# The first norm of five batches from an input with channels on partitions

## The chip, the cores and the metric

The kernel runs on one core of a Trainium2 chip. Time is the device time of one launch in microseconds (us). The core's engines are PE (TensorE, matmuls and transposes), DVE (VectorE), ACT (ScalarE), POOL (GpSimd) and SP (SyncE, which here only issues DMAs). "PEld" is the loading of weights into PE, which overlaps PE's matmuls.

## The reference

Eight batches of 256 tokens with 256 channels go through four layers in float32, each with a residual (`x = x + layer(x)`).

```
L0:  x = x + attention(norm1(x));  return x + swiglu(norm2(x))      16 heads of 16 channels, hidden 1024
     norm(x) = g * x * rsqrt(mean(x*x, channels) + 1e-6) + b,   g, b = linear maps of the batch's condition
L1:  attention with masked keys, then an RMS norm scaled and shifted by the condition
L2:  quaternion rotation; with the transform and its inverse it is one fixed 256 x 256 linear map
L3:  router over 8 experts, the best two; each expert is a network 256 -> 512 -> 512 -> 256
```

The change concerns `norm1` alone: the first norm of L0, for batches 3 to 7. Its mean runs over the channels of a token, so the divisor belongs to a token, while `g` and `b` belong to a channel of a batch.

## The kernel before, in words

**Layouts.** A batch `x` lies in SBUF with 128 tokens on the partitions and two token groups beside each other (128 x 2 x 256, `NQ` = 2). A matmul contracts over partitions, so the projections to queries, keys and values need the channels on partitions (`xT`, 128 x 2 x 256, `KC` = 2).

**The first norm** (`first_norm`, 1045, and `normed`, 891) works in the first layout: two Square activations on ACT with a running sum (`junk_n`, line 878), 11 small DVE instructions for the reciprocal root (`rq_..._n`, 611 to 622, no table), and two multiplications on POOL (`xs_n`, 902), one for each token group. It is a generator in three parts, which the caller starts one at a time. `first` (1053) then calls `conditioned` (908): four 128 x 128 transposes on PE (`flipped`, 884, `pt_n`) into one PSUM bank, and two DVE instructions (924) that read the bank and apply `g` and `b`, which in this layout are one number for each partition. Then come the projections (`qkv`, 937): `pk`, `pq`, `pv`, of 8 matmuls together 1.8 us each.

**Attention** has four score blocks for each batch and layer. A block (983 to 991) is four matmuls into one tile of four PSUM banks, `s_a`, and one exp on ACT over 128 x 2048 (`pe_a`, line 990). The pool of that tile has one buffer (531), so the next block's matmuls need the exp of the one before to be done. `values` (993) follows after every second block (`o_a`), with a transpose on DVE (`tu_a`). In this text `s_a_3_1_1` is the last of the four blocks of batch 3's first attention. All other results of PE go through three one-bank buffers (529).

**Order.** Batches 0 to 2 are set up first (to line 1824), with batch 3's first norm in `second_step` (1817). Then a loop for i from 2 to 6 (1829 to 1849) weaves, in each pass, eight score blocks: four of the second attention (L1) of batch i−2, then four of the first attention of batch i+1. Between the blocks `run` (1669) takes pieces from `others(i-1)` (1725): the SwiGLU of batch i−1 (`pg`, `ph`, then `pd`), with the pieces of `first(i+2)` inside, and the projections of the second attention of batch i−1 (`pk_a`, `pq_a`, `pv_a`, lines 932 and 962, from `x2T`, after another norm `n2` and its flips). A piece has a planned cost, 1.9 us unless it yields another number, and pieces are taken until their sum reaches the planned time between blocks (`gaps`). PE's order is that of this text, and so are DVE's and ACT's in the loop, all three engines' and POOL's before it. `starts` and `beside` list which parts of norms (`n1` is batch i+2's first norm), rotations and the router go to DVE, ACT and POOL at which block.

**Transfers.** SP loads `x` of batch b+3 in `after_first` (1071) and a row `mod` broadcast over the partitions in `swiglu` (1086, a ring of two buffers). The last third of the time belongs to the experts, with their weights streamed in; the change does not touch it.

## Time and profile before

| what | value |
|---|---|
| median of 3 runs | 714.43 us (713.82 to 716.17) |
| the profiled execution | 713.96 us |
| its span, first to last instruction | 712.2 us |
| PE busy | 698.3 us |
| DVE busy | 367.3 us |
| ACT busy | 256.7 us |
| POOL busy | 182.5 us |
| exp of one score block | 1877 ns, 64 of them |
| mean granted clock of PE | 0.995 |

A row of the timeline gives the start, the duration, the engine and line, the operation with output and input, the number of instructions, and in brackets how long the engine had been idle and who released it. Matmuls overlap at their ends, so the time of one piece of work is read from its start to the start of the next. A line of the waits names an engine's line, the instruction that it waited for, then the sum in us, the number of waits and the longest. In a DMA row stand the number of transfers, the size of one and the time from issue to landing.

### The profile page before, as it was taken

What the parts mean: (1) busy time and instruction counts of PE and PEld (TensorE: products, weight loads), DVE (VectorE), ACT (ScalarE), POOL (GpSimd) and SP (SyncE); (2) the same over time, 40 slices, a digit from 0 to 9 for tenths busy, and PEclk for the clock granted to TensorE, in tenths of its full rate; (3) what the DMA queues carried; (4) which work ended last, traced back from release to release, by engine and by line L of the source; (5) the groups of instructions that cost most, each with busy time, mean ns of one, the idle gap of its engine ahead of it and who ended that gap; (6) DMA issues with size and microseconds to landing.
All of it is one profiled execution on the core that took longest, in us unless ns stands there. A gap on an engine that the chain in (4) does not pass through costs nothing.

```text
span 712.2 us, 11237 instructions
## 1 busy us (share of the span) xinstructions
PE 698.3 (98%) x4300; PEld 536.7 (75%) x4300; DVE 367.3 (52%) x1165; ACT 256.7 (36%) x412; POOL 182.5 (26%) x219
## 2 busy tenths in 40 slices
PE   9999999999999999999999999999999999999994
PEld 7567776766766766766666786688888998989884
DVE  5447435575468585477584776688222222222221
ACT  4553345345355345355434235322211222221220
POOL 5302601101100140100220116224463333433113
PEclk9999999999999999999999999999999999999998
DMA  8500000000020000020000421736595765956512
GB/s 292 168 17 15 1 1 16 1 16 16 1 75 17 1 17 1 1 75 1 2 15 1 142 75 25 289 131 210 151 307 164 228 228 167 300 170 237 179 16 34
DMA packets 26624, 67.66 MB, mean 95 GB/s; under 512 B 8121, under 2 KB 20737, under 8 KB 24129
## 3 DMA queue, kind: packets, MB, share of 16 engines
q1 hardware_dynamic: 17712, 55.20, 22.3%
q0 software_dynamic: 8560, 11.46, 7.4%
q8 instruction: 36, 0.59, 0.3%
q14 instruction: 28, 0.22, 0.1%
q10 hardware_dynamic: 288, 0.18, 0.1%
HBM read 57.24 MB, written 9.59 MB: 94 GB/s over the span
## 4 chain that ended last, share of the span: by engine, by line
PE 91%; DVE 5%; ACT 1%; issue 1%; POOL 1%; DMA 0%; POOLq 0%; DVEq 0%; ACTq 0%
PE ph_a_rest L1492 13%; PE s_a L988 9%; PE pg L1096 8%; PE o_a L1001 8%; PE ph L1096 7%; PE pd L1109 7%; PE ph_s_sure L1492 6%; PE ph_a_p L1492 5%; PE pe_a_rest L1522 4%; PE pq_a L932 4%; PE pk_a L932 4%; PE py L1024 2%; PE pe_s_sure L1522 2%; PE pe_a_p L1522 2%; PE pv_a L962 2%; PE py L1142 2%
## 5 line engine op out<-in xcount | busy, mean ns | idle before, releaser
L990 ACT ACTIVATE pe_a<-s_a 128x2048 f32<-128x2048 f32 x64 | 120.1, 1877 | 107.9 <-PE s_a L988 107.7
L988 PE MATMUL s_a<-qz_a,kT_a 32*128 32x512 f32 x512 | 73.2, 639 | 1.6 <-DVE qz_a L946 1.0
L1492 PE MATMUL ph_a_rest<-h_a_rest,w_a_rest 128*128 128x256 f32 x288 | 63.7, 379 | 0.0
L1096 PE MATMUL pg<-xT_n,gate_wT 128*128 128x256 f32 x256 | 61.9, 385 | 0.0
L1001 PE MATMUL o_a<-pe_a,va 128*32 128x256 f32 x1024 | 61.9, 382 | 0.0
L1096 PE MATMUL ph<-xT_n,hid_wT 128*128 128x256 f32 x256 | 61.6, 383 | 0.0
L1001 PEld LDWEIGHTS o_a<-pe_a,va 128*32 128x32 f32 x1024 | 30.0, 109 | 39.9 <-issue 23.4
L1492 PEld LDWEIGHTS ph_a_rest<-h_a_rest,w_a_rest 128*128 128x128 f32 x288 | 54.1, 190 | 7.0
L1109 PE MATMUL pd<-out_wT,hT 128*128 128x256 f32 x256 | 59.2, 383 | 0.0
L1096 PEld LDWEIGHTS ph<-xT_n,hid_wT 128*128 128x128 f32 x256 | 47.7, 190 | 13.7 <-DVE y L1068 3.0
L1109 PEld LDWEIGHTS pd<-out_wT,hT 128*128 128x128 f32 x256 | 47.7, 190 | 12.3 <-issue 3.2
L1096 PEld LDWEIGHTS pg<-xT_n,gate_wT 128*128 128x128 f32 x256 | 47.4, 190 | 12.1 <-issue 2.5
L1503 DVE TENSOR_SCALAR h_a_rest<-ph_a_rest,w_a_rest 128x256 f32<-128x256 f32 x36 | 17.4, 484 | 73.5 <-PE ph_a_rest L1492 72.4
L1069 POOL TENSOR_TENSOR xy<-y,x 128x512 f32<-128x512 f32 x8 | 10.1, 1268 | 143.1 <-DVE y L1068 88.1
L1501 ACT ACTIVATE h_a_rest<-ph_a_rest,w_a_rest 128x256 f32<-128x256 f32 x36 | 17.1, 475 | 77.3 <-DVE h_a_rest L1503 77.3
L1010 DVE STREAM_TRANSPOSE tu_a<-o_a 128x512 f32<-128x512 f32 x32 | 22.8, 712 | 40.6 <-PE o_a L1001 40.5
L1282 POOL DMA_INDIRECT slots<-rec,posi x32 | 31.8, 995 | 31.8 <-DVE rec L1280 16.5
L1536 POOL DMA_INDIRECT out<-ye_a_rest,trec_a_rest x18 | 28.5, 1581 | 39.1 <-ACT ye_a_rest L1534 30.0
L1100 ACT ACTIVATE th<-pg 128x512 f32<-128x512 f32 x32 | 19.0, 595 | 45.8 <-PE pg L1096 45.4
L988 PEld LDWEIGHTS s_a<-qz_a,kT_a 32*128 32x128 f32 x512 | 20.2, 183 | 19.5 <-issue 12.8
L1102 DVE SCALAR_TENSOR_TENSOR sg<-th,pg 128x512 f32<-128x512 f32 x32 | 21.9, 684 | 24.0 <-ACT th L1100 24.0
L1492 PE MATMUL ph_a_rest<-xt_a_rest,w_a_rest 128*128 128x256 f32 x144 | 32.6, 379 | 0.0
(354 smaller groups left out, 1176.1 us busy)
## 6 DMA issues: line engine op xcount, KB each, us to landing
w_a_rest<-in_experts SPq DMA_DIRECT2D x9, 2180.0 KB, 9.2
w_a_p<-in_experts SPq DMA_DIRECT2D x5, 2180.0 KB, 8.7
w_s_sure<-in_experts SPq DMA_DIRECT2D x4, 2180.0 KB, 9.3
w_s_early<-in_experts SPq DMA_DIRECT2D x1, 2180.0 KB, 8.4
mod<-mod_rows SPq DMA_DIRECT2D x8, 256.0 KB, 3.3
tokens<-x SPq DMA_DIRECT2D x4, 512.0 KB, 3.2
out<-x SPq DMA_DIRECT2D x4, 512.0 KB, 4.4
x<-in_x SPq DMA_DIRECT2D x7, 256.0 KB, 2.7
```

The costliest lines, as they stand in the source:

```text
L932: nc.tensor.matmul(pp[:, c, :], w[:, k, c * P : (c + 1) * P], xT[:, k, :], start=k == 0, stop=k == KC - 1)
L988: nc.tensor.matmul(sc[:, j], kT[r, c, kc * P : (kc + 1) * P], qz[r, c], start=True, stop=True)
L990: nc.scalar.activation(pe, sc, AF.Exp)
L1001: nc.tensor.matmul(o[32 * i : 32 * i + 32, qd, :], va[:, kc, 8 * c + 4 * qd + i].rearrange("p a d -> p (a d)"), pe[:, 2 * qd + i // 2, i % ...
L1010: nc.vector.transpose(turned.rearrange("p q j a d -> p (q j a d)"), o.rearrange("p q s -> p (q s)"))
L1096: nc.tensor.matmul(ps[:, j, :], w[:, k, o : o + P], yT[:, k, :], start=k == 0, stop=k == KC - 1)
L1102: nc.vector.scalar_tensor_tensor(sg, th, 1.0, pg, ALU.add, ALU.mult)
L1109: nc.tensor.matmul(pd[:, t, :], hT[:, c, t * P : (t + 1) * P], out_w[:, c, :], start=c == 0, stop=c == HID // P - 1)
L1282: sc = nc.gpsimd.indirect_dma_start(out=slots, out_offset=bass.IndirectOffsetOnAxis(ap=posi[:, t : t + 1], axis=0), in_=rec[:, t, :], in_o ...
L1492: nc.tensor.matmul(ph[:, c - c0, 0:many], w[:, o : o + P], src[:, k, 0:many], start=k == 0, stop=k == n_in - 1,)
L1522: nc.tensor.matmul(pos[q][0:p, q, :], h2[:, k, q * p : (q + 1) * p], w[:, o : o + D], start=k == 0, stop=k == MC - 1,)
L1536: ad = nc.gpsimd.indirect_dma_start(out=out[0 : reach(n), :], out_offset=bass.IndirectOffsetOnAxis(ap=rec[0:p, q, 0:1], axis=0), in_=y[0:p ...
```

## The change

The host adds a second copy of `x` with channels on partitions. For batches 3 to 7 `first_turned` takes the place of `first_norm`: the squares and the reciprocal root are as before, but the scaling by the root works on the turned copy. There the divisor runs along a row, the same for all partitions, so the 256 roots are written to DRAM and read back as one row broadcast to 128 partitions. DVE multiplies the turned copy by it, POOL applies `g` and `b`, and `first` goes to the projections without transposes. The piece that held the flips stays in the plan with a cost of 0.0 instead of 0.6. In the loop the parts of `n1` start two blocks earlier, and in `second_step` the first two parts of batch 3's norm come one step earlier. The tile `scaled` moves to the ring of `mod`. The planned `gaps` stay as they are.

```diff
+    rstd_rows = dram.tile([B, P, NQ], F32, tag="rstd_rows", name="rstd_rows")
...
-        scaled = work.tile([P, KC, B, E], F32, tag="r_msg", bufs=1, name="scaled")
+        scaled = wt("mod", [P, KC, B, E], "scaled")
...
+    def first_turned(b):
+        s = state[b]
+        s["x"] = xs_in.pop(b)
+        ss = squares(s["x"], f"n1_{b}")
+        xT = wt("xs", [P, KC, S], f"xr_{b}", 3)
+        nc.sync.dma_start(out=xT, in_=a["xT"][b])
+        yield
+        rstd = rsqrt(work, ss, NQ, 1.0 / D, 1e-6, f"n1_{b}")
+        nc.sync.dma_start(out=rstd_rows[b], in_=rstd)
+        rows_ = wt("rb", [P, P, NQ], f"rb_{b}", 1)
+        nc.sync.dma_start(
+            out=rows_.rearrange("p t q -> p (t q)"),
+            in_=rstd_rows[b].rearrange("t q -> (t q)").partition_broadcast(P),
+        )
+        yield
+        parts = xT.rearrange("p k (q t) -> p k q t", q=NQ)
+        nc.vector.tensor_tensor(
+            parts, parts, rows_.rearrange("p t q -> p q t").unsqueeze(1).to_broadcast([P, KC, NQ, P]), ALU.mult
+        )
+        dst = s["xT1"] = wt("xT", [P, KC, S], f"xT_n1_{b}", 3)
+        for k in range(KC):
+            nc.gpsimd.tensor_scalar(
+                dst[:, k, :], xT[:, k, :], aff[:, 0, k, b : b + 1], aff[:, 1, k, b : b + 1], ALU.mult, ALU.add
+            )
+        yield
+
     def first(b):
         s = state[b]
+        if "xT1" in s:
+            yield 0.0
+            s["qkv0"] = yield from qkv(s.pop("xT1"), wq0, wk0, wv0, f"a0_{b}")
+            return
...
+            n1 = first_turned(3)
+            next(n1)
+            next(n1)
             next(rotation)
             yield
-            do(first_norm(3))
+            do(n1)
...
-        n1 = first_norm(i + 2) if i + 2 < B else iter(())
+        n1 = first_turned(i + 2) if i + 2 < B else iter(())
...
-        starts = {0: [last], 1: [last, n2], 2: [n2, n1]}
+        starts = {0: [last, n1], 1: [last, n2], 2: [n2]}
         beside = {
-            0: [last], 1: [last, n2], 2: [n1, n1], 3: [last], 4: [placed], 5: [r1], 6: [rotated],
+            0: [last, n1], 1: [last, n2], 2: [n1], 3: [last], 4: [placed], 5: [r1], 6: [rotated],
...
+        "xT": v["x"].transpose(0, 2, 1).reshape(B, KC, P, S).transpose(0, 2, 1, 3),
```

## The prediction

> **What bounds the kernel now.** I read the page's first part, the slices and the chain, then the waits of TensorE (PE), then its timeline around each place that the change touches.

> ```profile
> PE 698.3 (98%) x4300; PEld 536.7 (75%) x4300; DVE 367.3 (52%) x1165; ACT 256.7 (36%) x412; POOL 182.5 (26%) x219
> ...
> PEclk9999999999999999999999999999999999999998
> ...
> PE 91%; DVE 5%; ACT 1%; issue 1%; POOL 1%; DMA 0%; POOLq 0%; DVEq 0%; ACTq 0%
> ```

> PE is busy for 698.3 of 712.2 us at an undiminished clock, and 91% of the chain is its own work. So a change pays what it takes off PE's text order, and costs what it makes PE wait. PE has few waits (columns: us in all, times, longest):

> ```profile
> PE pt_n L888 <- POOL xs_n L902: 0.6, 1, 0.6
> ...
> PE s_a L988 <- ACT pe_a L990: 0.2, 1, 0.2
> ```

> The second line is the rule that decides this case. All score blocks share one PSUM tile, and the next block's first matmul needs the last exp (`pe_a`) to have emptied it. PE's timeline (start, duration, count) in one pass of the steady loop, and ScalarE's (ACT) exp in it:

> ```profile
> 147.87 1.14 PE L988 MATMUL s_a<-qz_a,kT_a 32*128 32x512 f32 x8
> 148.94 2.05 PE L962 MATMUL pv_a<-wv,x2T 128*128 128x264 f32 x8
> 151.01 1.14 PE L988 MATMUL s_a<-qz_a,kT_a 32*128 32x512 f32 x8
> 152.08 1.93 PE L1001 MATMUL o_a<-pe_a,va 128*32 128x256 f32 x32
> ```

> ```profile
> 149.08 1.88 ACT L990 ACTIVATE pe_a<-s_a 128x2048 f32<-128x2048 f32 x1 [3.37 <-PE s_a L988]
> ```

> From 147.87 to 151.01 are 3.14 us: 1.07 of scores (start to next start), 0.14 until the exp begins, 1.88 of exp, 0.05 until PE goes on. The matmuls between (`pv_a`) took 2.07 where they take 1.88 elsewhere (95.53 to 97.41), so PE already stood 0.19 there. The same 3.14 to 3.15 stands at 201.47, 256.32, 309.92 and 352.40, whatever lies between, and where the 1.86 of `o_a` lies between, the wait is named:

> ```profile
> 439.93 1.93 PE L1001 MATMUL o_a<-pe_a,va 128*32 128x256 f32 x32
> 442.05 1.14 PE L988 MATMUL s_a<-qz_a,kT_a 32*128 32x512 f32 x8 [0.19 <-ACT pe_a L990]
> ```

> So 3.14 is the least distance of two score blocks.

> **What the change removes: the flips.** Four transposes for each of batches 3 to 7, on PE's path. From their start to the next one's: batch 3 0.49 (81.47 to 81.96), batches 4, 5 and 7 0.53 each (126.83, 180.44, 288.89), batch 6 1.38, with the wait on POOL in it:

> ```profile
> 228.76 5.45 PE L1109 MATMUL pd<-out_wT,hT 128*128 128x256 f32 x24
> 234.07 0.33 PE L888 MATMUL pt_n<-ident,xs_n 128*128 128x128 f32 x1
> 234.97 0.55 PE L888 MATMUL pt_n<-ident,xs_n 128*128 128x128 f32 x3 [0.57 <-POOL xs_n L902]
> 235.45 1.14 PE L988 MATMUL s_a<-qz_a,kT_a 32*128 32x512 f32 x8
> ```

> Sum 3.46. Two waits go as well in batch 3's stretch: `pk_a` on the scale and shift after the flips (step 2.07 at 81.96 instead of 1.83: 0.24), and at 89.47 the wait for `x2T` (again 2.07 for 1.83: 0.24), since the order now has `pt_x_0` one score block earlier. Gain: 3.46 + 0.24 + 0.24 = **3.94 us**. The two L924 instructions of a batch (0.99 together) leave VectorE (DVE) and hide beside PE now; I count nothing.

> **What it moves on PE: the pieces.** The loop places pieces of work between score blocks by planned costs. The flips' piece was planned at 0.6; now it is 0.0, so one more piece fits ahead of a block. By the two orders of PE, in the four passes with a batch to load (i = 2 to 5), `pd` becomes one run ahead of `s_a` 0_0, and `pt_x`, `py`, `pv`, `pt_n2`, `pq_a1` and `pv_a1` all go ahead by one block. Behind the last block of batch i+1 (`s_a_3_1_1` to `s_a_6_1_1`) nothing is left: the next block of the other attention (`s_a_1_0_0` to `s_a_4_0_0`) follows directly. By the 3.14 PE then stands 3.14 − 1.07 = 2.07 four times. `pv_a1` (1.88), which filled that place, is now paid ahead of it: 4 × 1.88 = **7.5 us lost**. Bounds: 7.1 with the quickest row of that form (1.78); nothing if the scores did not wait for the exp, which the 0.19 at 442.05 excludes; no gain, since no matmul went away there. I take 7.5.

> The clock: after a 0.98 wait ahead of 363.09 PE has its full clock.

> ```profile
> 360.00:363.00 3.00, 2.11 (x10) 1.47 (x8) 2.86 (x10) 0.95 (x2) 1.93 (x4) 1.00 0.02 1
> ```

> (Busy us of PE, its loads, DVE, ACT, POOL; then the granted clock, 1.00.) [...]

> **What it moves on DVE.** `first_turned` starts two blocks earlier, so the 11 small instructions of the reciprocal root (2.11 us) stand right after `y` of batch b−2. In passes 2, 3 and 5 DVE has idle time behind. In pass 4 it is the middle of the router's chain, without a gap from 215.37 to 228.8, and `hT` is late behind it:

> ```profile
> 215.56 1.26 DVE L617 TENSOR_SCALAR rq_y_r<-rq_v_r 128x4 int32<-128x4 int32 x1
> ...
> 230.10 0.69 DVE L1104 TENSOR_TENSOR hT<-sg,ph 128x512 f32<-128x512 f32 x1
> ```

> That `hT` is ready at 230.8 now; 2.11 more, less the 0.55 of idle ahead of 229.31, makes 232.3. `pd` (from 228.76) wants it at its seventh pair, 6 × 0.44 = 2.65 later: 231.4. I take **0.9 us** (bounds 0 and 1.5, the whole of the 2.11 less the present 0.6 slack).

> The first line also shows a small DVE instruction at 1.26 (0.17 elsewhere) while POOL adds `xy` (1.26 from 215.53). [...]

> **What it adds: the row through DRAM.** Nearest rows (KB, median us to landing):

> ```profile
> mod<-mod_rows SPq DMA_DIRECT2D x8, 256.0 KB, 3.3
> ...
> trec_s_sure<-slots SPq DMA_DIRECT2D x4, 4.0 KB, 1.9
> aff_w<-in_aff_w SPq DMA_DIRECT2D x2, 128.0 KB, 5.0
> ```

> The write (1 KB) I take at 1.9 and up to 3.3, the broadcast read back, of `mod`'s size and form, at 3.3. Batch 3: root done at 72.85 (it follows another root on DVE, which ends at 70.74), row in DRAM at 74.8 to 76.2, back at 78.1 to 79.5, DVE multiply 0.69, POOL 0.92 + 0.92: `xT` at 80.6 to 82.1. `pk_3` wants it at 83.3 (83.79 less the flips): slack 1.2 or more. DVE waits up to 4 us at the multiply; behind it `hall`, `each` and `tu` queue, wanted at 81.6 at the earliest (`tu`, idle 2.74 ahead of it). POOL's fill of `va` behind it slips by the same, to 90.5 for a copy at 97. Batches 4 to 7: root done some 9 us ahead of the multiply (121.3 for batch 4), the trip takes 5.2 to 6.6, so no wait. On SP the write waits for the root and the read for the write; queued behind them are `mod` and the next `x`, wanted tens of us later. `scaled` takes a buffer of `mod`'s ring, so `mod_1` loads only after `phall` (78.4) and lands by 82, wanted near 133. The `xT` load (2.7 by the row of `x`) goes out a batch ahead. All costed at **0**; its cover is the slack named, and at 5.0 a transfer (the `aff_w` row) batch 3 alone would be late, by about 2.

> **Sum.** −3.94 + 7.5 + 0.9 = +4.5 on the profiled 713.96 (span 712.2 and 1.76 around it): 718.4. The median of the runs is 0.47 above that execution; I say **718.7**, between the two ways of counting it.

> **Rivals.** A change below 0.3%, 2.1 us, is about what these runs cannot tell from none.
> 1. *The likeliest*: four bare exps, 716.5 to 720.5. Chance 0.62.
> 2. *Faster: the gap is not paid.* The place is `s_a_3_1_1` to `s_a_1_0_0`: if what I read in the order is not what runs there, or the 2.07 pays waits that stand elsewhere, such as late DVE work, 713.96 − 3.94 + 0.9 = 710.9, or 710.0 without the DVE term. For it: PE has 14 us of idle in all, some of it owed to other engines. Against it: five spacings of 3.14. It turns faster when a gap nets under 0.76 of its 1.88 ((3.94 − 0.9)/4). Chance 0.10.
> 3. *Late row.* Batch 3's trip at 10 us: DVE multiplies at 83.5, `xT` at 85.4 for 83.3, +2; if the other four slip too (9 us of lead, so 1 to 2 each), up to +8: 720.5 to 727. For it: writes of 8 bytes a partition have no row here. Against it: the 1.9 of `trec`. Chance 0.12.
> 4. *Clock.* If PE ran slower behind each gap and lost as much again as the gap, 4 × 2.07: 726.7. Against it the window at 360. Chance 0.05.
> 5. *Within noise*: the gap is half covered, +0.5 or so: 714.5. Chance 0.11.

> Faster 0.10, same 0.11, slower 0.79. The range: 714.5 (case 5) to 723 (the lesser half of case 3) leaves out about 0.18.

> **What would show it.** The waits of PE in the changed profile: `s_a <- ACT pe_a` four times at 2.0 each (8 in all) if I am right; `pk_a` or `pd` waiting on `xT_n` or on DVE's multiply if the row is late; `pd <- DVE hT` near 232 for the DVE term; no `pt_n` of batches 3 to 7 and 40 instead of 60 of them. Wrong would be a PE sum of waits under 4, or granted clock below 0.99 behind the gaps.

## The result and the profile after

The changed kernel takes 723.39 us (median of 4 runs, 723.31 to 724.39) against 714.47 for the kernel before in the same comparison: ratio 1.0135, interval 1.0113 to 1.0156. The prediction said 718.7 and 714.5 to 723.0: the right sign, twice too small a loss. The profiled execution took 723.38 with a span of 721.7, against 713.96 and 712.2.

The page of the changed kernel, first part and chain:

```profile
PE 699.7 (97%) x4280; PEld 535.8 (74%) x4280; DVE 368.4 (51%) x1160; ACT 258.6 (36%) x412; POOL 178.5 (25%) x219
...
PE 90%; DVE 5%; ACT 2%; DMA 1%; issue 1%; POOL 0%; SPq 0%; POOLq 0%; DVEq 0%; ACTq 0%
```

PE has 20 instructions fewer and yet is busy 1.4 us longer than before, although the flips alone should have taken away some 3. So PE must be slower somewhere, not only later. The waits of PE (us in all, times, longest):

```profile
PE s_a L989 <- ACT pe_a L991: 8.2, 5, 2.0
...
PE pd L1142 <- DVE hT L1137: 0.4, 1, 0.4
```

These two are the ones that the prediction named: the exp ahead of the score blocks, four times 2.0 on top of the 0.2 of before, and one late `hT`. They explain 4 × 1.88 and 0.4, not the rest. The timeline of PE around the first of the four gaps:

```profile
147.86 1.14 PE L989 MATMUL s_a<-qz_a,kT_a 32*128 32x512 f32 x8
150.99 1.89 PE L989 MATMUL s_a<-qz_a,kT_a 32*128 32x512 f32 x8 [2.00 <-ACT pe_a L991]
152.81 2.82 PE L1002 MATMUL o_a<-pe_a,va 128*32 128x256 f32 x32
155.56 2.00 PE L1129 MATMUL pg<-xT_n,gate_wT 128*128 128x256 f32 x8
```

The block after the gap takes 1.82 from start to start instead of 1.07, and `o_a` 2.75 instead of 1.86: 1.64 lost behind the gap, with nothing to wait for. The windows view shows a lower clock there. Each pair below is the stretch of 3.41 us that holds a gap and the one behind it, for the first, the second and the fourth gap (busy us of PE, its loads, DVE, ACT and POOL, then the granted clock, share of DMA, GB/s):

```profile
147.84:151.25 3.41, 1.41 (x13) 0.57 (x16) 3.31 (x11) 2.35 (x2) 0.00 (x0) 1.00 0.26 77
151.25:154.67 3.42, 3.42 (x28) 1.00 (x28) 3.32 (x6) 1.68 (x1) 0.00 (x0) 0.50 0.03 5
205.87:209.28 3.41, 1.61 (x20) 0.68 (x24) 3.31 (x9) 2.09 (x2) 0.00 (x0) 1.00 0.10 35
209.28:212.69 3.41, 3.41 (x38) 2.42 (x31) 3.27 (x7) 3.31 (x9) 0.00 (x0) 1.00 0.04 12
318.51:321.92 3.41, 1.48 (x16) 0.60 (x20) 3.29 (x9) 2.09 (x2) 0.00 (x0) 1.00 0.20 44
321.92:325.33 3.41, 3.41 (x33) 1.59 (x22) 2.90 (x5) 3.31 (x8) 0.00 (x0) 0.50 0.00 0
```

Where the span's 9.4 us went, by the starts of the score blocks behind the four gaps:

| stretch ending at the block of before / after | before | after | difference | made of |
|---|---|---|---|---|
| 78.53 / 78.33 | 78.53 | 78.33 | −0.20 | start |
| 151.01 / 150.99 | 72.48 | 72.66 | +0.18 | gap +1.88; flips of batches 3 and 4 −1.02; two waits −0.48; −0.2 in `pk`, `pq` |
| 204.62 / 207.67 | 53.61 | 56.68 | +3.07 | gap +1.88; half clock +1.64; flips −0.53 |
| 259.46 / 263.77 | 54.84 | 56.10 | +1.26 | gap +1.88; late `hT` +0.7; flips −1.38 |
| 313.06 / 320.44 | 53.60 | 56.67 | +3.07 | gap +1.88; half clock +1.64; flips −0.53 |
| end of the span | 399.2 | 401.2 | +2.0 | half clock +1.64; 0.4 among the experts |

The last 0.4 stands also in a kernel without the new row (256.6 from the last score block to the end in "order alone" below, 256.3 before, 256.6 after), so I don't count it as the new row's.

### The profile page after: what moved, and what is told of

Same layout as the page of the kernel before. It is cut to its first block, busy times and chain, and to the rows that moved or that the text cites. A ratio compares the mean times of both kernels' runs of the same rounds, so it can differ in the third digit from the quotient of the medians.

```text
span 721.7 us, 11208 instructions
## 1 busy us (share of the span) xinstructions
PE 699.7 (97%) x4280; PEld 535.8 (74%) x4280; DVE 368.4 (51%) x1160; ACT 258.6 (36%) x412; POOL 178.5 (25%) x219
## 4 chain that ended last, share of the span: by engine, by line
PE 90%; DVE 5%; ACT 2%; DMA 1%; issue 1%; POOL 0%; SPq 0%; POOLq 0%; DVEq 0%; ACTq 0%
PE ph_a_rest L1525 13%; PE s_a L989 9%; PE o_a L1002 8%; PE pg L1129 8%; PE pd L1142 8%; PE ph L1129 7%; PE ph_s_sure L1525 6%; PE ph_a_p L1525 5%; PE pe_a_rest L1555 4%; PE pk_a L933 4%; PE pq_a L933 3%; PE py L1025 2%; PE pe_s_sure L1555 2%; PE pe_a_p L1555 2%; PE pv_a L963 2%; ACT pe_a L991 2%
## 5 line engine op out<-in xcount | busy, mean ns | idle before, releaser
L989 PE MATMUL s_a<-qz_a,kT_a 32*128 32x512 f32 x512 | 74.8, 653 | 9.7 <-ACT pe_a L991 8.2
L1002 PE MATMUL o_a<-pe_a,va 128*32 128x256 f32 x1024 | 64.9, 396 | 0.0
## 6 DMA issues: line engine op xcount, KB each, us to landing
mod<-mod_rows SPq DMA_DIRECT2D x8, 256.0 KB, 3.2
x<-in_x SPq DMA_DIRECT2D x7, 256.0 KB, 2.7
```

Of the source, the lines that this page charges most:

```text
L989: nc.tensor.matmul(sc[:, j], kT[r, c, kc * P : (kc + 1) * P], qz[r, c], start=True, stop=True)
L1002: nc.tensor.matmul(o[32 * i : 32 * i + 32, qd, :], va[:, kc, 8 * c + 4 * qd + i].rearrange("p a d -> p (a d)"), pe[:, 2 * qd + i // 2, i % ...
```

## The experiments

Two theories: **order and clock** (the gaps that the new order of PE leaves cost 1.88 each and, where a gap lies badly, 1.64 of half clock) and, as rival, **the new row** (its trip through DRAM and its DVE and POOL work cost what the waits don't explain). The ratios are to the kernel before in the same comparison.

**The slot's planned cost put back.**

```diff
         if "xT1" in s:
-            yield 0.0
+            yield 0.6
```

> The changed kernel with the planned cost of the empty piece put back from 0.0 to 0.6, and nothing else. That returns PE's order to that of before without the flips: the projection pv_a1 stands between the last block of one attention and the first of the other again. Theory (order and clock): the four waits of 2.0 on the exp go, and with them the three stretches at half clock of 1.64 each: 723.4 - 4 x 1.88 - 3 x 1.64 = 711.0, ratio to before 0.995. Rival (the new row through DRAM, or POOL and DVE work, costs the part that the four waits don't explain): 723.4 - 7.5 = 715.9, ratio 1.002.

Measured: 712.01 against 715.02, ratio 0.9954 (0.9937 to 0.9971). PE's order is that of before again, with `pv_a` in the old place:

```profile
144.69 1.14 PE L989 MATMUL s_a<-qz_a,kT_a 32*128 32x512 f32 x8
145.76 2.05 PE L963 MATMUL pv_a<-wv,x2T 128*128 128x264 f32 x8
147.83 1.14 PE L989 MATMUL s_a<-qz_a,kT_a 32*128 32x512 f32 x8
148.90 1.93 PE L1002 MATMUL o_a<-pe_a,va 128*32 128x256 f32 x32
```

One number turned a loss of 1.35% into a gain of 0.46%. The row, the turned input and the missing flips are all still there, so the new row is not where the time went. This version is ahead of both kernels, each time by more than the intervals leave open.

**The order alone**, on the kernel before: flips, norms and transfers as they were.

```diff
-        yield 0.6
+        yield 0.0 if b >= 3 else 0.6
         s["qkv0"] = yield from qkv(xT, wq0, wk0, wv0, f"a0_{b}")
```

> The kernel before with only the planned cost of the flips' piece of batches 3 to 7 set from 0.6 to 0.0; flips, norms and transfers stay. Theory (order and clock): four waits of 2.0 on the exp appear, +7.5, less the 0.24 of the wait for x2T, and some of the four gaps lower the clock at 1.64 each: 721.2 with none, 722.9 to 727.8 with one to four, ratio 1.010 to 1.019. Rival (the row through DRAM costs what the waits don't explain): no drop of the clock, 721.2, ratio 1.010.

Measured: 725.08, ratio 1.0147 (1.0123 to 1.0171). So the loss exists without any of the new operations. Its waits and the stretches at its second gap:

```profile
PE s_a L988 <- ACT pe_a L990: 8.2, 5, 2.0
```

```profile
206.38:209.80 3.42, 1.42 (x20) 0.52 (x20) 3.28 (x10) 1.97 (x2) 0.00 (x0) 1.00 0.28 59
209.80:213.21 3.41, 3.41 (x33) 1.53 (x26) 2.78 (x5) 3.31 (x8) 0.00 (x0) 0.50 0.00 0
```

Here the second and the third gap lowered the clock, the first and the fourth did not.

**The gaps filled.** In the changed kernel, matmuls of the identity in each of the four gaps, whose result nobody reads; first eight, then two.

```diff
+        if second and (c, kc) == (0, 0) and 1 <= b <= 4:
+            keep_busy(8, f"pw_{b}")
         live[layer, b].scores(c, kc)
```

> The changed kernel with eight 128x128 matmuls of the identity (about 1.0 us, their result is read by nobody) in each of the four gaps. Theory (an idle gap of 2.06 lowers the clock for 3.41 us): the distance of the two score blocks stays 3.14, the wait falls to about 1.0, and no stretch at half clock is left behind the gaps: 723.4 - 4.9 = 718.5, ratio 1.006. Rival (the half clock has another cause, or costs nothing): 723.4, ratio 1.0125.

Measured: 718.35, ratio 1.0050 (1.0032 to 1.0068). My length for the filler was wrong: eight of them took 2.06, not 1.0, so they filled the whole gap.

```profile
148.12 1.14 PE L989 MATMUL s_a<-qz_a,kT_a 32*128 32x512 f32 x8
149.19 2.05 PE L1804 MATMUL pw<-ident 128*128 128x128 f32 x16
151.25 1.14 PE L989 MATMUL s_a<-qz_a,kT_a 32*128 32x512 f32 x8
152.32 1.93 PE L1002 MATMUL o_a<-pe_a,va 128*32 128x256 f32 x32
```

The two blocks still stand 3.13 apart, so no work was moved or made quicker; PE only did nothing useful instead of nothing. The median fell by 5.0 from the 723.39 (6.1 by the two ratios); three times 1.64 is 4.9. The blocks and `o_a` behind the gap are back at 1.07 and 1.86.

> As with eight, but two such matmuls (0.27 us), so that PE is idle for about 1.8 in each gap. Theory (what counts is the idle time within one of the 3.41 us stretches in which the clock is judged; 1.80 idle in one kept the clock at the second gap, 1.93 lowered it at the fourth): no or one drop, 718.5 to 720.1, ratio 1.006 to 1.008. Rival (any gap of this kind lowers the clock): 723.4.

Measured: 718.46, ratio 1.0053 (1.0033 to 1.0073); two fillers took 0.65 and left 1.35 idle, where I had reckoned with 1.8. The profiled execution (717.15, among the shortest of the seven) has no stretch at half clock in the loop. Only two of its four gaps lie whole in one stretch; the first of these two, with the stretch behind:

```profile
258.83:262.24 3.41, 2.06 (x20) 0.89 (x20) 3.27 (x9) 1.88 (x1) 1.68 (x6) 1.00 0.32 74
262.24:265.65 3.41, 3.41 (x42) 2.33 (x40) 3.34 (x6) 2.78 (x5) 0.00 (x0) 1.00 0.02 5
```

So 1.35 idle in one stretch kept the clock, twice in one execution. Where the border lies this run does not show.

**Which gaps lower the clock.** Both kernels once more, for more gaps.

> The changed kernel once more, for a second profile of its four gaps. Theory (the clock is judged in fixed stretches of 3.41 us, whose position against the kernel differs from execution to execution; a stretch with more than 1.80 to 1.93 us of idle PE halves the clock in the next): some of the four gaps lower the clock, not the same ones as in the first profile; each that does has 1.9 or 2.0 of its idle time in one stretch, each that doesn't has 1.8 or less. Rival (it depends on what work stands around the gap): the first, third and fourth gap again, the second not.

> The kernel before with the cost 0.0, once more. The same two theories: by the first, gaps with 1.9 or more idle in one stretch lower the clock and the others don't; by the rival the second and third gap again, the first and fourth not.

These two and all that follow ran on another chip, on which every kernel is 20 to 26 us slower, the one before too (738.5 to 740.1): in several places DVE and ACT stand idle for 3 to 8 us with no releaser that the profile can name (DVE 7.65 ahead of 258.38 and ACT 6.36 ahead of 258.63 in the version with the cost put back), PE waits for them (4.71 ahead of 269.48 in the changed kernel), and the clock drops there as well: the score block behind that wait takes 2.09 instead of 1.14. Why is open. The two are single executions, of 745.04 and 745.01. One gap of each lies inside such a place and is left out. The first gap (151.18 to 153.18) and the second (207.89 to 209.89) of the changed kernel there, each with the stretch behind:

```profile
150.86:154.27 3.41, 1.41 (x15) 0.33 (x11) 3.27 (x9) 1.88 (x1) 0.00 (x0) 1.00 0.18 65
154.27:157.68 3.41, 3.41 (x36) 1.36 (x32) 2.83 (x5) 2.78 (x5) 0.00 (x0) 0.50 0.03 5
205.47:208.89 3.42, 2.42 (x15) 1.12 (x13) 3.28 (x9) 1.88 (x3) 0.00 (x0) 1.00 0.28 68
208.89:212.30 3.41, 2.41 (x35) 1.14 (x39) 3.34 (x8) 2.09 (x2) 0.00 (x0) 1.00 0.04 13
```

All 14 gaps of 2.00, with the larger part of each that lies in one stretch of the grid (which each execution's own stretches at half clock fix):

| execution | clock halved behind it | clock kept |
|---|---|---|
| changed, first profile | 2.00, 2.00, 1.93 | 1.80 |
| order alone, first | 2.00, 2.00 | 1.19, 1.47 |
| changed, again | 2.00 | 1.00, 1.61 |
| order alone, again | 2.00 | 1.36, 1.50 |

The same gap of the same kernel falls on either side (the second and fourth do so in "order alone", the fourth in the changed kernel), and the idle time in one stretch sorts all 14. The rival, that the work around a gap decides, is out. The border holds for these gaps. In the disturbed places of the second chip some stretches with less recorded idle were followed by half clock too (1.36 in the changed kernel, from 454.65), but there the record draws matmuls out over a pause (a score block of 3.19 instead of 1.14), so the idle time can't be read.

**What the trip through DRAM costs.** On the version with the cost put back, run once more beside these:

> The same kernel as the one with the planned cost put back to 0.6, run again beside the next three, so that they are compared on one chip. Expected 712.0, between 709.6 (no stretch at half clock in the set-up) and 712.4, ratio 0.995.

Measured: 735.86 against 740.06, ratio 0.9943 (0.9920 to 0.9966): the ratio holds on this chip, the times don't. Next the row from a table that is ready long before; the divisor is left out of the result:

```diff
+        rows_ = wt("rb", [P, P, NQ], f"rb_{b}", 1)
+        nc.sync.dma_start(
+            out=rows_.rearrange("p t q -> p (t q)"), in_=mod_rows[b, 0 : P * NQ].partition_broadcast(P)
+        )
         yield
...
-        rows_ = wt("rb", [P, P, NQ], f"rb_{b}", 1)
-        nc.sync.dma_start(
-            out=rows_.rearrange("p t q -> p (t q)"),
-            in_=rstd_rows[b].rearrange("t q -> (t q)").partition_broadcast(P),
-        )
         yield
```

> The kernel with the cost put back to 0.6, but the row is read from another table in DRAM that is ready long before, together with the turned input, so nothing waits for the root and its trip; the root is still written to DRAM, and what it divides by is left out of the result. Theory (the trip is covered): DVE's wait of 6.5 to 7.2 at batch 3's multiply goes, the time stays at 712.0, within 0.5. Rival (the trip costs PE something the waits don't show): 711 or less.

Measured: 736.96, ratio 0.9958 (0.9945 to 0.9970), not faster than with the trip (0.9943, the intervals overlap); DVE multiplies at 74.23, 7.9 earlier than with the trip on the same chip (82.08). In the times the wait cost nothing that can be seen. In the profile it cost half a us in batch 3: from the start of the `pd` ahead of `pk` to `pq` are 4.04 with the trip (81.45 to 85.49) and 3.56 without (81.73 to 85.29), though no wait bears that name.

And one more hop:

```diff
-        nc.sync.dma_start(out=rstd_rows[b], in_=rstd)
+        nc.sync.dma_start(out=rstd_hop[b], in_=rstd)
+        nc.sync.dma_start(out=rstd_rows[b], in_=rstd_hop[b])
```

> The kernel with the cost put back to 0.6, with one more hop for the roots, from DRAM to DRAM (1 KB, about 3 us by the write's 3.1). Theory (batch 3 has hardly any slack, batches 4 to 7 have several us): xT of batch 3, ready 0.7 ahead of its use now, comes 2.3 late, pk waits that long once, the others do not: 712.0 + 2.3 = 714.3, ratio 0.9985. Rival (the trip has the slack of 1.2 or more that the prediction gave it, and more): 712 to 713.8; rival (all five are at the edge): 5 x 2.3, 723.

Measured: 737.54, ratio 0.9976 (0.9955 to 0.9998). PE in batch 3's stretch:

```profile
81.82 1.99 PE L1144 MATMUL pd<-out_wT,hT 128*128 128x256 f32 x8
84.89 2.10 PE L934 MATMUL pk_a<-xT_n,L_WkT 128*128 128x256 f32 x8 [1.08 <-POOL xT_n L1079]
```

`pk` waits once, 1.1 where I expected 2.3, since the trip grew by only 1.0 (root's end to the multiply 10.25, against 9.27 without the hop on this chip). The other four batches don't wait. So batch 3 stands at the edge (on this chip 0.5 behind it already without the hop) and the others have room, as expected; the whole median moved by 1.7, more than the wait, and the intervals overlap.

**The roots half a pass ahead**, on the version with the cost put back.

```diff
-        n1 = first_turned(i + 2) if i + 2 < B else iter(())
+        if i == 2:
+            n1 = first_turned(4)
+        else:
+            n1 = ahead
+        ahead = first_turned(i + 3) if i + 3 < B else iter(())
...
+        if i > 2:
+            starts[0], beside[0] = [last], [last]
+        beside[5].append(ahead)
+        beside[6].append(ahead)
```

> The kernel with the cost put back to 0.6, with squares, root and trip of batches 5 to 7 half a pass earlier (at the sixth and seventh block of the pass before), so that the 11 root instructions of batch 6 no longer stand in the router's chain on DVE. Theory (pd waits for hT because of them): the wait of 0.42 on hT goes, the time falls by 0.4 to 0.7, to 711.4, ratio 0.9945. Rival (DVE's queue is late there anyway, or is late at the new place): the wait stays or moves, 712.0 or more.

Measured: 736.14, ratio 0.9937 (0.9912 to 0.9962). Without it on this chip, then with it:

```profile
226.43 1.14 PE L989 MATMUL s_a<-qz_a,kT_a 32*128 32x512 f32 x8
227.50 2.86 PE L1142 MATMUL pd<-out_wT,hT 128*128 128x256 f32 x12
230.77 2.86 PE L1142 MATMUL pd<-out_wT,hT 128*128 128x256 f32 x12 [0.41 <-DVE hT L1137]
233.56 1.14 PE L989 MATMUL s_a<-qz_a,kT_a 32*128 32x512 f32 x8
```

```profile
228.00 1.14 PE L989 MATMUL s_a<-qz_a,kT_a 32*128 32x512 f32 x8
229.07 5.45 PE L1142 MATMUL pd<-out_wT,hT 128*128 128x256 f32 x24
234.44 1.14 PE L989 MATMUL s_a<-qz_a,kT_a 32*128 32x512 f32 x8
```

From block to block 7.13 became 6.44: the late `hT` cost 0.69 (0.41 of it under that name). The mechanism is shown in the profile; in the time 0.1% is too little to see.

> The kernel with the cost put back and the roots of batches 5 to 7 half a pass earlier, once more, for its interval: 0.9937 to 0.995 of the time before.

Measured: 734.89 against 738.53, ratio 0.9946 (0.9926 to 0.9966). It beats the kernel before, as the version it is built on does; the two can't be told apart.

## Why the prediction was wrong

- **The flips and two waits, −3.94**: right. The stretches without a gap's clock agree within 0.3, and with the order restored the kernel is 0.46% faster, 3.3 of 715 (2.1 to 4.5), where −3.94 and the 0.7 of DVE make −3.2 (−3.0 without the wait for `x2T`, which that order brings back).
- **Four bare exps, +7.5**: right. Four waits of 2.00, the blocks 3.13 to 3.14 apart; the order alone brings them.
- **DVE's root in the router's chain, +0.9**: right in kind, 0.7 in size. Of POOL's work, the scale and shift (1.09 from 81.90) overlap DVE in batch 3 alone, and nothing is drawn out there (`tu_a` 0.69, its mean is 0.71). Beside `xy` the root is drawn out: in batches 4, 5 and 7 it now starts there (`xy` 1.26 or 1.27 from 106.87, 163.55 and 276.32), and one of its instructions takes 1.26 or 1.27 instead of 0.17 and ends within 0.03 of that, as the router's did before. PE waited for none of the three.

```profile
106.90 1.26 DVE L618 TENSOR_SCALAR rq_y_n<-rq_v_n 128x2 int32<-128x2 int32 x1
```

- **The clock, taken at 0**: this is the step that failed, the reading that a gap of 2.07 leaves PE its full clock. In the profiled execution three of the four gaps halved the clock for 3.41 us, and each cost 1.64: 4.9 us, as much again as the rest of the sum (+4.5 predicted, +8.9 measured in the medians). The prediction had it as a rival with a chance of 0.05, priced as "as much again as the gap", and its own sign of being wrong, a granted clock below 0.99 behind the gaps, is what came (0.50).

One thing stays open. Two of the other three executions took the same time (723.31 and 723.40) with a mean clock of 0.992 instead of 0.986. They lost some 4 us less of clock, the worth of two to three such stretches (1.7 each), one of which may lie behind the last matmul and cost nothing. Either they were slower for another reason, or their clock is not fully on record; there is no trace of them. So the count of three holds for the profiled execution alone. That the idle time of the gaps costs some 5 us beside the 7.5 rests on the filled kernels, which need no clock record.

The reason given was one row: full clock behind a wait of 0.98. But the row shown, 360 to 363, ends before that wait does (363.09); the stretch behind it does have the full clock, and that shows nothing for a gap of twice the length. And the profile of before had a row that speaks against it, which the prediction passed over; the slices of the page round it to a 9. These are two stretches in the set-up of the kernel before, and the matmuls that fill most of the first:

```profile
32.57:35.98 3.41, 3.29 (x24) 2.92 (x23) 2.64 (x7) 0.00 (x0) 0.00 (x0) 1.00 0.00 0
35.98:39.39 3.41, 3.41 (x9) 2.68 (x9) 0.00 (x0) 0.59 (x1) 0.00 (x0) 0.50 0.02 5
```

```profile
32.80 1.95 PE L758 MATMUL pgconst<-small_in,cond_b 64*128 64x8 f32 x16
```

A full 3.41 us at half clock in the middle of a stream of matmuls, behind a stretch with many small ones (16 of 64x8). It says that the clock can fall in this kernel and that it takes no long pause; with it the rival would have deserved an even chance, and the range an upper end near 725 (718.4 and four times the 1.64 measured later). In the profiled execution of the first experiment the same matmuls (32.60 to 34.55) are cut by a line of the grid, at 33.25, and the clock stays:

```profile
33.25:36.67 3.42, 3.30 (x21) 2.98 (x21) 1.82 (x5) 0.00 (x0) 0.00 (x0) 1.00 0.02 5
36.67:40.08 3.41, 3.41 (x19) 2.12 (x18) 0.69 (x1) 1.45 (x5) 0.91 (x1) 1.00 0.00 0
```

`pk` and `py` behind them took 3.62 together instead of 5.31, and the execution was the fastest of its seven (709.63, median 712.01). All thirteen traces go the same way. In ten the 1.95 us of these matmuls lie in one stretch (1.93 in one trace), with little other idle, and the clock halves behind it. In the three others the larger part is 1.29, 1.30 and 1.67, and it does not. With these matmuls, 8 columns wide, counted as idle, the stretches come to 1.99 or more in the ten and 1.79 or less in the three, the same border as for the gaps. That is read off the traces; no run was made to test it.

- **The row through DRAM, 0**: right in the time, but by luck in its parts. The trip took 8.4 in batch 3 (the root's end at 72.6, the multiply at 81.03) and not 5.2 to 6.6: the 1 KB write took 4.9 there, and the row 3.5 from the issue of its read to the multiply. (In the other batches the write takes 3.0 to 3.2; where the broadcast's landing is on record it took 4.1 to 4.7.) POOL's two instructions made up for it with 0.55 each instead of 0.92:

```profile
L1077 POOL TENSOR_SCALAR xT_n<-xr,aff 128x256 f32<-128x256 f32 x10 | 5.4, 553 | 66.9 <-DVE wo L1697 41.1 <-PE o_a L1002 13.3 <-PE s_a L989 12.5
...
rb<-rstd_rows SPq DMA_DIRECT2D x5, 128.0 KB, 4.6
...
rstd_rows<-rq_y_n SPq DMA_DIRECT2D x5, 1.0 KB, 3.1
```

`xT` of batch 3 was ready at 82.99 for a `pk` at 83.10: a slack of 0.1 where the prediction had 1.2 or more.

## What to carry to other kernels

Where a planner places work by costs, taking an operation away moves everything behind it: read the order of the critical engine between the two instructions that share a buffer, because the piece that stood there may have been hiding the wait, and keep the planned cost of the removed piece until the order has been looked at. A gap on PE is not priced at its length alone: ask the granted clock at a fine step over the whole kernel before taking it as constant, and count what a stretch at half clock cost here (1.64 us) for each gap behind which the clock may fall. A removal that gains 3 us and a placement that loses some 12 can hide in one diff; run them apart.

## What the hardware showed that I had not expected

- The three stretches at half clock in the loop of the changed kernel lie on one grid of 3.4133 us; of 14 gaps of 2.00 us in four executions the 7 with 1.93 or more in one stretch were followed by half clock in the next, the 7 with 1.80 or less were not. Recorded idle time is not the whole measure: in the set-up of before a stretch with 0.12 us idle was followed by half clock. It fits the same border if its 16 matmuls of 64x8 (1.95 us) count as idle, and so do the set-ups of all 13 traces.
- The mean granted clock of an execution does not order its time: the four of the changed kernel read 0.986, 0.992, 0.988 and 0.992 at 723.38, 723.31, 724.39 and 723.40. I have the trace of the first alone, so this stays open, and with it how many stretches at half clock the other three had.
- POOL's multiply and add with two numbers for each partition took 553 ns for 128x256, its multiply alone 919 to 923 for the same size (`xs_n`). I did not test why.
- A 1 KB write from SBUF, 8 bytes a partition, took 3.0 to 4.9 us to land on SP's queue, no less than `x`'s loads of 256 KB (2.7).
